# Two graph-attention layers on one core: the order of score and attention products in a step, some moved work in the opening, and the banks of the last row

## The chip, the cores and the metric

The kernel runs on one core of a Trainium2 chip. A core has five engines that run at the same time, each through its own queue in order: TensorE (PE in the profile; its weight loads are shown apart as PEld), VectorE (DVE), ScalarE (ACT), GpSimd (POOL) and SyncE (SP), which here issues the transfers between the chip's memory (DRAM) and the on-chip buffer. Matrix products land in PSUM, a small memory of eight banks for accumulation; everything else lives in the on-chip buffer of 128 partitions. The metric is the device time of the kernel in microseconds (us). A shorter time is better.

## The reference, cut to what matters

The input is x, 128 graphs of 128 nodes with 512 features each, and adj, a 128 by 128 mask for each graph. Two layers follow one another. Each is masked attention over the nodes, a residual addition and a layer normalisation:

```
x = layernorm(x + attention_0(x, adj))   # 4 heads of 64, no norm before, mask = adj
x = layernorm(x + attention_1(x, adj))   # 8 heads of 64, layernorm with gamma and beta before, mask = adj or self
attention: q, k, v = x W;  s = q k^T / 8;  s = where(mask, s, -big);  p = softmax(s);  out = (p v) Wo + bias
```

Everything is float32.

## The kernel before, in words

**Tiling.** Two graphs make a group, so there are 64 groups (NG). One group's 256 rows go through layer 0 and some steps later through layer 1. All products with weight matrices use a seven-product scheme for two-by-two blocks (Strassen's): seven half-size products, numbered 1 to 7, in place of eight, paid for with sums and differences of blocks. `sums` (L312) and `out_sums` make those of the rows on GpSimd (line 324), `weight_sums` (L202, `combine` at L211, line 214) those of the weights, once. A product accumulates into one of three PSUM banks, called a, c and f after the table `INTO`, and products 1, 6, 7, 4 follow one another in bank a, 5 and 3 in bank f. Between two of them an engine reads the bank: a product that goes on in a bank must wait until the earlier value has been read.

**Steps.** The program is written out as one sequence, and each engine gets its instructions in that order; nothing reorders them. `opening` (L809) loads and transposes weights and takes groups 0 and 1 through the first stages. `step(s)` (L852) then runs for s = 2 to 63, and `closing_a`, two of `closing_b` and `last` finish the pipeline. A step works on several groups at once, which are at different stages: the layer 0 projections of group s (`product_0`, line 477), the scores of group s-1 in layer 0 (part 0) and of group s-4 in layer 1 (parts 1 and 2, one per graph), the attention products of group s-2 in layer 0 (part 0) and s-5 in layer 1 (parts 1 and 2), the layer 1 projections of group s-3 (`qk` and `v`, line 361), and the output projections of groups s-2 and s-5 (`out_product`, line 517). Parts 1 and 2 of the attention products therefore exist from step 5 on.

**Scores and attention products.** `scores` (L532) makes eight short products a part (16 records in the profile, two for each product): q of 64 features by k of 64 features, so that only 64 of the array's rows are used; even heads use the upper half, odd heads the lower. Part 0 is line 550; parts 1 and 2 are line 556. Parts 0 and 2 take two PSUM banks each from a pool of four (tag mm), part 1 takes the banks a0 and f0. `attend` (L656, products on line 679) multiplies the probabilities with v, again in eight products a part: here 128 rows are used but 64 columns. Part 0 goes to bank a, part 1 to bank f, part 2 to one of the pool. ScalarE copies the results out (lines 682 and 684). For the step the order of these products is:

```
made = scores(s, 0)
attend(s, 1)
made.update(scores(s, 1, 2))
...
attend(s, 0, 2)
```

`masked` (line 585, VectorE) writes the scores where the mask is set, `maxima` (line 591, VectorE) takes the row maxima, `exps` (line 600, ScalarE) the exponentials and their sums, `normalised` (lines 608 and 609, VectorE and GpSimd) divides, and `blocks` and `probs_arrive` turn the probabilities over through DRAM for the next step; `blocks_direct` (L642) does that on TensorE instead. `with_self` (L561, line 564) adds the diagonal to the mask for layer 1.

**What comes into the scores of layer 1.** Queries and keys of a group are written to DRAM and fetched back in another order by `kq_arrive` (L417) at the end of a step. `q_in_order` (L422, line 426) then has ScalarE copy the queries of both graphs into the tiles qo0 and qo1, and the next step's parts 1 and 2 of the scores read them.

**Residual rows.** `addend` (L694, line 701, GpSimd) adds a bias to the rows of a group, `out_product` adds the projections to them on VectorE (line 521), `stats` and `roots` make mean and scale (lines 712 to 735), and `flush` (L57) emits the normalisations that were queued (line 746, ScalarE).

**The end.** For the last group, `out_plain` (L760, line 769) makes each graph's output rows as two plain halves of 256 columns, both in one PSUM bank; `add_plain` (L772, lines 779 and 780) adds each half to the row and takes its statistics, `root_plain` and `norm_plain` (lines 784 to 793) finish and store the row.

Of the kernel before, what the change touches and what calls it, by code (L numbers as in the profile page):

```python
# [10 lines left out]
F32 = mybir.dt.float32  # L11
# [6 lines left out]
P = 128  # L18
# [9 lines left out]
def kernel(ctx: ExitStack, tc: tile.TileContext, x, adj, wq, wk, wv, wo, bo,  # L28
                            gamma, beta, w_qkv, w_out, b_out, out):
    nc = tc.nc  # L30
# [15 lines left out]
    ps_st = ctx.enter_context(tc.tile_pool(name="ps_st", bufs=1, space=PSUM))  # L46
# [97 lines left out]
    wo1 = const.tile([P, INNER[1] // P, E], F32, name="wo1")  # L144
# [167 lines left out]
    def sums(l, g):  # L312
        if not 0 <= g < NG:
            return
        xs = XS[l, g] = one.tile([P, 4, KH, N], F32, tag=f"xs{l}", name=f"xs{l}_{g}")
        halves_sums(xs, XT[l, g].rearrange("p (h c) (b n) -> p b h c n", h=2, b=2))
# [10 lines left out]
    XS, ACC, EV = {}, {}, {}  # L327
# [197 lines left out]
    SM, TOTAL, NMAX, PT, AT, SO = {}, {}, {}, {}, {}, {}  # L525
# [6 lines left out]
    def scores(s, *parts):  # L532

        made = {}
        for part in parts or PARTS:
            g = group_of(s, part)
            if g is None:
                continue
            if part == 1:
                ps = [ps_st.tile([P, 512], F32, tag=t, name=f"sc{part}_{g}_{t}") for t in ("a0", "f0")]  # L540
            else:
                ps = [mm_tile(f"sc{part}_{g}_{i}") for i in range(2)]
            ps = [x.rearrange("p (k n) -> p k n", n=N) for x in ps]
            if part == 0:
                for b in range(G):
                    for h in range(HEADS[0]):
                        r = slice((h % 2) * D, (h % 2 + 1) * D)
                        k_ = (qkv0[r, b, h // 2, 2].rearrange("p (a j) -> p a j", j=32) if g in PLAIN_0 else
                              RAW[0][r, :, 1, b * K0 + h // 2])
                        nc.tensor.matmul(ps[h % 2][:, b * K0 + h // 2, :].rearrange("p (a j) -> p a j", j=32),  # L550
                                         qkv0[r, b, h // 2, 1], k_, start=True, stop=True)
            else:
                b = part - 1
                for h in range(HEADS[1]):
                    r = slice((h % 2) * D, (h % 2 + 1) * D)
                    nc.tensor.matmul(ps[h % 2][:, h // 2, :].rearrange("p (a j) -> p a j", j=32),  # L556
                                     QO[g, b][r, h // 2], KQ[r, :, 0, b, h // 2], start=True, stop=True)
            made[part] = ps
        return made

    def with_self(g):  # L561

        if 0 <= g < NG:
            nc.vector.tensor_tensor(M[g], M[g], eye[:, None, :].to_broadcast([P, G, N]), op=ALU.max)
# [29 lines left out]
    def exps(s, part, *halves):  # L594
        if group_of(s, part) is None:
            return
        sm, nmax, total = SM[part], NMAX[part], TOTAL[part]
        for i in halves:
            for k in range(K1):
                nc.scalar.activation(sm[:, i, k, :], sm[:, i, k, :], AF.Exp, bias=nmax[:, i, k:k + 1],  # L600
                                     accum_out=total[:, i, k:k + 1])
# [158 lines left out]
    def out_plain(g, b, *steps):  # L760

        n = E // 2
        if 0 in steps:
            ACC["op", b] = ps_st.tile([P, 512], F32, tag=("a0", "f0")[b], name=f"op_{b}")
        acc = ACC["op", b]
        for i in steps:
            h = slice(i * n, (i + 1) * n)
            for c in range(K1):
                nc.tensor.matmul(acc[:, h], AT[1, g][:, b, c], wo1[:, c, h], start=i == 0 and c == 0,
                                 stop=c == K1 - 1, skip_group_check=True)  # L770

    def add_plain(g, b, i):  # L772

        n = E // 2
        h = slice(i * n, (i + 1) * n)
        row = R[g][:, b, h]
        if i == 0:
            ST[b] = two.tile([P, 2, nc.vector.BN_STATS_DIM], F32, tag="st_last", name=f"st_last{b}")
        nc.vector.tensor_add(row, ACC["op", b][:, h], row)
        nc.vector.bn_stats(ST[b][:, i], row)  # L780

    def root_plain(b):
# [26 lines left out]
    def opening():  # L809

        sums(0, 0)
        cleared(1, 0)

        for t in (1, 0, 2):
            if t == 0:
                for h in range(2):
                    nc.vector.tensor_scalar_mul(w0[:, :, 0, h, :], w0[:, :, 0, h, :], SCALE)
            product_0(0, 1, 2, ts=(t,))
            weight_sums_0(t)
        product_0(0, 5, 6, 3)  # L820
        prepare(2)
        load(2)
        product_0(0, 7)
        prepare(2)
        product_0(0, 4)
        transposed(1)
        load_quarters(2)
        sums(0, 1)

        made = scores(1)  # L830
        masked(made, 1, 0)
        maxima(1, 0)
        weight_sums_out(0)
        product_0(1, 1, 2)
        exps(1, 0, 0, 1)
        prepare(2)
        normalised(1, 0)
        product_0(1, 6, 5)
        prepare(2)
        addend(0, 0)  # L840
        product_0(1, 7)
        prepare(2)
        blocks_direct(1, 0)
        cleared(2, 0)
        weight_sums(w1qk, wsqk, 0)
        product_0(1, 3)
        prepare(2)
        product_0(1, 4)
        transposed(2)
        sums(0, 2)  # L850

    def step(s):  # L852

        made = scores(s, 0)
        attend(s, 1)
        made.update(scores(s, 1, 2))
        if s > 3:
            sums(0, s)
            arrive(s - 3)
        flush()  # L860
        load_ahead(s + 1)
        load_rows(s - 1)
        masked(made, s, 0, 1, 2)
        attend(s, 0, 2)
        maxima(s, *((0,) if s == 4 else (0, 1)))
        if s == 3:
            turn(s - 3)
            arrive(s - 3)
        out_sums(0, s - 2)
        if s == 3:  # L870
            sums(0, s)
            with_self(s - 3)
        exps(s, 0, 0)
        product_0(s, 1)
        exps(s, 0, 1)
        out_product(0, s - 2, 1, 2, *(() if s == 2 else (5,)))
        maxima(s, *((1, 2) if s == 4 else (2,)))
        product_0(s, 2)
        if s == 2:
            out_product(0, s - 2, 5, 6)  # L880
        normalised(s, 0)
        out_product(0, s - 2, *(() if s == 2 else (6,)), 3)
        exps(s, 1, 0)
        stats(0, s - 2, 0)
        product_0(s, 6)
        exps(s, 1, 1)
        out_product(0, s - 2, 7)
        (blocks_direct if s == 2 else blocks)(s, 0)
        product_0(s, 5)
        out_product(0, s - 2, 4)  # L890
        normalised(s, 1)
        finish(s - 3, 0)
        stats(0, s - 2, 1)
        exps(s, 2, 0)
        product_0(s, 7)
        finish(s - 3, 1)
        exps(s, 2, 1)
        if s > 2:
            probs_arrive(s, 0)
        blocks(s, 1)  # L900
        product_0(s, 3)
        if s == 3:
            weight_sums(w1qk, wsqk, 1)
        product_0(s, 4)
        transposed(s + 1)
        turn_qk0(s)
        if s in (2, 3):
            prepare(len(setup) - (s == 2))
        normalised(s, 2)
        qk(s - 3, 1)  # L910
        if s == 2:
            prepare(1)
        flush()
        if s > 2:
            probs_arrive(s, 1)
        qk(s - 3, 2)
        blocks(s, 2)
        arrive_qk0(s)
        qk(s - 3, 6)
        if s == 3:  # L920
            weight_sums(w1v, wsv, 0)
        if s == 4:
            weight_sums_out(1)
        qk(s - 3, 5)
        flush(latest)
        addend(1, s - 5)
        out_sums(1, s - 5)
        qk(s - 3, 7)
        if s == 3:
            weight_sums(w1v, wsv, 1)  # L930
        qk(s - 3, 3, 4)
        kq_arrive(s - 3)
        probs_arrive(s, 2)
        out_product(1, s - 5, 1, 2)
        v(s - 3, 1, 2)
        if s > 2:
            turn(s - 2)
        cleared(s + 1, 0, 1, 2)
        v(s - 3, 6)
        out_product(1, s - 5, 6, 5)  # L940
        v(s - 3, 5)
        out_product(1, s - 5, 7, 3, 4)
        q0_in_order(s)
        q_in_order(s - 3)
        addend(0, s - 1)
        v(s - 3, 7)
        stats(1, s - 5, 0)
        v(s - 3, 3)
        stats(1, s - 5, 1)
        v(s - 3, 4)  # L950
        if s > 2:
            with_self(s - 2)
        if s == NG - 1:
            arrive(s - 2)
            addend(1, s - 4)
# [162 lines left out]
    for s in range(2, NG):  # L1118
        step(s)
# [33 lines left out]
```

## Time and profile before

| | us |
|---|---|
| median of 3 runs | 2761.13 (2759.78 to 2761.82) |
| the profiled execution's own time | 2759.77 |
| its span, first to last instruction | 2758.0 |
| TensorE busy (PE) | 2743.3 |
| VectorE busy | 2033.5 |
| GpSimd busy | 1752.0 |
| ScalarE busy | 1506.1 |
| granted TensorE clock, share of full | 0.999 |

Times in the profile are counted from the first instruction. A row of the timeline gives start, duration, engine, line, operation, result and operands by the program's names, shapes (for a product: the size of the stationary operand, then the moving one) and how many records it joins; a bracket at its end says how long the engine had been idle before and what released it. Ends of matrix products are modelled by the profiler, so their starts are the better clock: the time of a stage below is the distance from its first start to the next stage's first start. The step s = 33, in the middle of the run, starts its scores at 1315.74 and the next step at 1358.23; periods of 42.49 and 42.35 us alternate from step 5 to step 62.

### The profile page before, as it was taken

Reading aid. Unit: us, or ns where it says so; the run is one execution under the profiler, and the core shown is the slowest. Engines: PE = TensorE matmul, PEld = TensorE weight load, DVE = VectorE, ACT = ScalarE, POOL = GpSimd, SP = SyncE. Lnnn points to the kernel's source line nnn. Section 1 sums busy time; section 2 is a strip of 40 time slices with the busy share of each in tenths; the row PEclk is TensorE's granted clock in tenths of the full one; section 3 lists DMA queues with packets and bytes.
Section 4 is the critical chain, followed back from the end, with each engine's and each line's share of the span. In section 5 each row is a group of like instructions: output and inputs, shape, how many; then the busy total and the mean of one; then the engine's idle time right before and its main releaser. Section 6 shows DMA issues by size and latency. Waiting matters only on the chain.

```text
span 2758.0 us, 49315 instructions
## 1 busy us (share of the span) xinstructions
PE 2743.3 (99%) x15811; PEld 2032.5 (74%) x15811; DVE 2033.5 (74%) x3671; ACT 1506.1 (55%) x4804; POOL 1752.0 (64%) x2311
## 2 busy tenths in 40 slices
PE   9999999999999999999999999999999999999998
PEld 8867767677776677776776767777767777677688
DVE  6777777777777777777777777777777777777765
ACT  3456465464564654645646546456465464564654
POOL 5565666666656666666566666665666666656664
PEclk9999999999999999999999999999999999999999
DMA  6567777777777777777777777777777777777652
GB/s 179 154 200 206 218 217 204 218 210 215 212 202 219 216 204 219 210 216 209 205 217 217 204 219 210 214 213 203 216 218 203 215 214 215 211 204 220 201 150 65
DMA packets 550290, 562.73 MB, mean 204 GB/s; under 512 B 55560, under 2 KB 468752, under 8 KB 550032
## 3 DMA queue, kind: packets, MB, share of 16 engines
q1 hardware_dynamic: 550032, 559.58, 71.5%
q8 instruction: 127, 2.08, 0.3%
q14 instruction: 131, 1.07, 0.1%
HBM read 300.95 MB, written 258.47 MB: 203 GB/s over the span
## 4 chain that ended last, share of the span: by engine, by line
PE 97%; DMA 1%; DVE 1%; issue 0%; SPq 0%; ACT 0%; POOL 0%; POOLq 0%; DVEq 0%; ACTq 0%
PE qka L361 16%; PE a L477 12%; PE oa L517 12%; PE va L361 8%; PE qkf L361 8%; PE av L679 7%; PE f L477 6%; PE of L517 6%; PE vf L361 4%; PE qkc L361 4%; PE oc L517 3%; PE c L477 3%; PE sc L550 2%; PE sc_a L556 2%; PE sc L556 2%; PE vc L361 2%
## 5 line engine op out<-in xcount | busy, mean ns | idle before, releaser
L600 ACT ACTIVATE sm<-sm,nmax 128x128 f32<-128x128 f32 x1536 | 594.8, 391 | 30.6 <-DVE nmax L591 27.9
L609 POOL TENSOR_TENSOR sm<-sm,rec 128x1024 f32<-128x1024 f32 x192 | 364.1, 1896 | 333.7 <-DVE rec L608 330.7
L701 POOL TENSOR_TENSOR r<-r,bias 128x1024 f32<-128x1024 f32 x128 | 301.5, 2356 | 130.9 <-ACT r L700 130.9
L521 DVE TENSOR_TENSOR r<-oa,r 128x256 f32<-128x256 f32 x508 | 211.1, 415 | 134.9 <-PE oa L517 129.4
L600 ACT ACTIVATION_READ_ACCUMULATOR sm<-sm,nmax 128x1 f32 x1536 | 291.4, 190 | 0.0
L371 ACT COPY ev<-va 128x256 f32<-128x256 f32 x128 | 47.6, 372 | 432.8 <-PE va L361 432.8
L627 DVE STREAM_TRANSPOSE turnedp<-sm 128x1024 f32<-128x1024 f32 x188 | 233.6, 1243 | 64.5 <-POOL sm L609 53.9
L720 POOL TENSOR_SCALAR ve<-mv 128x2 f32<-128x2 f32 x191 | 41.7, 218 | 371.4 <-DVE mv L713 360.9
L591 DVE TENSOR_REDUCE nmax<-sm 128x8 f32<-128x1024 f32 x192 | 226.6, 1206 | 0.3
L361 PE MATMUL qkf<-w,xs 128*128 128x512 f32 x472 | 221.8, 592 | 0.0
L361 PE MATMUL qka<-wsqk,xs 128*128 128x512 f32 x472 | 221.8, 592 | 0.0
L517 PE MATMUL of<-wo,so 128*128 128x256 f32 x760 | 205.9, 379 | 1.4 <-DVE r L521 1.0
L517 PE MATMUL oa<-wso,so 128*128 128x256 f32 x760 | 206.0, 380 | 0.4 <-DVE r L521 0.4
L324 POOL TENSOR_TENSOR xs<-xT 128x256 f32<-128x256 f32 x256 | 187.7, 733 | 22.4 <-DVE xT L118 18.6
L746 ACT ACTIVATE r<-r,shift,root 128x512 f32<-128x512 f32 x254 | 193.0, 809 | 2.5 <-POOL shift L735 2.5
L426 ACT ACTIVATE qo<-kq 128x512 f32<-128x512 f32 x118 | 67.9, 622 | 228.6 <-DMA kq<-scrkq 228.6
L324 POOL TENSOR_TENSOR so<-aT 128x256 f32<-128x256 f32 (+1 forms) x254 | 150.2, 591 | 52.1 <-ACT aT L682 44.6
L477 PE MATMUL f<-w,xs 128*128 128x128 f32 (+1 forms) x760 | 182.2, 376 | 0.2 <-DVE w L214 0.2
L477 PE MATMUL a<-ws,xs 128*128 128x128 f32 (+1 forms) x760 | 182.1, 375 | 0.0
L585 DVE COPY_PREDICATED sm<-m,sc 128x512 f32<-128x512 uint8 x256 | 172.4, 727 | 11.1 <-PE sc L550 2.2
L712 DVE BATCH_NORM_STATS2 st<-r 128x6 f32<-128x512 f32 x254 | 174.9, 689 | 2.3
L571 POOL MEMSET sm<- 128x1024 f32 x192 | 175.1, 952 | 1.4 <-DVE turnedp L627 1.4
(181 smaller groups left out, 6471.9 us busy)
## 6 DMA issues: line engine op xcount, KB each, us to landing
scrp<-turnedp SPq DMA_DIRECT2D x188, 512.0 KB, 3.6
pT<-scrp SPq DMA_DIRECT2D x752, 128.0 KB, 2.9
kq<-scrkq SPq DMA_DIRECT2D x236, 256.0 KB, 4.8
x<-in_x_dram SPq DMA_DIRECT2D x256, 128.0 KB, 4.0
r<-in_x_dram SPq DMA_DIRECT2D x64, 512.0 KB, 4.0
out_dram<-r SPq DMA_DIRECT2D x63, 512.0 KB, 3.6
scr<-turned SPq DMA_DIRECT2D x62, 512.0 KB, 6.7
kq<-scr SPq DMA_DIRECT2D x248, 128.0 KB, 2.8
```

The source lines that it names most:

```text
L324: nc.gpsimd.tensor_tensor(o, a0, a1, op=op)
L361: nc.tensor.matmul(o, lhsT, rhs, start=first and m == 0, stop=m == len(todo) - 1, skip_group_check=True)
L477: nc.tensor.matmul(o, lhsT, rhs, start=first and n == 0, stop=n == len(todo) - 1, skip_group_check=True)
L517: nc.tensor.matmul(acc, left[:, c], right[:, c], start=first and c == 0, stop=c == hk - 1, skip_group_check=True)
L521: nc.vector.tensor_add(part, acc, part)
L591: nc.vector.tensor_reduce(NMAX[part], SM[part], AX.X, ALU.max, negate=True)
L600: nc.scalar.activation(sm[:, i, k, :], sm[:, i, k, :], AF.Exp, bias=nmax[:, i, k:k + 1], accum_out=total[:, i, k:k + 1])
L609: nc.gpsimd.tensor_tensor(SM[part], SM[part], rec[:, :, :, None].to_broadcast([P, 2, K1, N]), op=ALU.mult)
L627: nc.vector.transpose(t.rearrange("p q (h r) -> p q h r", r=32), SM.pop(part).rearrange("p i k (q r) -> p q (i k) r", r=32))
L679: nc.tensor.matmul(pm[i * D:(i + 1) * D, at, :].rearrange("p (a r) -> p a r", r=32), v, pT[:, :, i * K1 + at, :], start=True, stop=True)
L701: nc.gpsimd.tensor_tensor(R[g], R[g], (bias0, bias1)[l][:, None, :].to_broadcast([P, G, E]), op=ALU.add)
L746: nc.scalar.activation(R[g][:, b], R[g][:, b], AF.Identity, bias=shift[:, b:b + 1], scale=root[:, b:b + 1])
```

## The change

In each step all score products of the three parts are now issued first, and all attention products of the three parts after them, in the place where parts 0 and 2 stood. In the queues of the other engines this moves the copy of part 1 (line 684) behind the normalisations that `flush` emits and behind part 0's copy.

In the first steps several pieces of work have other places: the sums of group 2's rows (from the end of `opening` into step 2, behind `out_sums`), the diagonal of group 0's mask (from the first half of step 3 to its end), the exponentials of part 0 (in steps 2 to 4 behind the first projection product with its copy), the maxima of part 2 in step 4, `blocks_direct` in step 2, and the bias addition of group 2 in step 3.

At the end, the two halves of each of the last rows go to two PSUM banks each, so that the four halves use a0, a, f0 and f.

```diff
     def out_plain(g, b, *steps):
         n = E // 2
-        if 0 in steps:
-            ACC["op", b] = ps_st.tile([P, 512], F32, tag=("a0", "f0")[b], name=f"op_{b}")
-        acc = ACC["op", b]
         for i in steps:
-            h = slice(i * n, (i + 1) * n)
+            acc = ACC["op", b, i] = ps_st.tile([P, 512], F32, tag=(("a0", "a"), ("f0", "f"))[b][i], name=f"op_{b}{i}")
             for c in range(K1):
-                nc.tensor.matmul(acc[:, h], AT[1, g][:, b, c], wo1[:, c, h], start=i == 0 and c == 0,
+                nc.tensor.matmul(acc[:, :n], AT[1, g][:, b, c], wo1[:, c, i * n:(i + 1) * n], start=c == 0,
                                  stop=c == K1 - 1, skip_group_check=True)
...
-        nc.vector.tensor_add(row, ACC["op", b][:, h], row)
+        nc.vector.tensor_add(row, ACC["op", b, i][:, :n], row)
...
         prepare(2)
         product_0(1, 4)
         transposed(2)
-        sums(0, 2)
 
     def step(s):
-        made = scores(s, 0)
-        attend(s, 1)
-        made.update(scores(s, 1, 2))
+        made = scores(s)
...
         masked(made, s, 0, 1, 2)
-        attend(s, 0, 2)
+        attend(s)
...
         out_sums(0, s - 2)
-        if s == 3:
+        if s in (2, 3):
             sums(0, s)
-            with_self(s - 3)
-        exps(s, 0, 0)
+        if s > 4:
+            exps(s, 0, 0)
         product_0(s, 1)
-        exps(s, 0, 1)
+        exps(s, 0, *((0, 1) if s < 5 else (1,)))
         out_product(0, s - 2, 1, 2, *(() if s == 2 else (5,)))
-        maxima(s, *((1, 2) if s == 4 else (2,)))
+        maxima(s, 1 if s == 4 else 2)
...
         exps(s, 1, 0)
+        if s == 4:
+            maxima(s, 2)
         stats(0, s - 2, 0)
         product_0(s, 6)
         exps(s, 1, 1)
         out_product(0, s - 2, 7)
-        (blocks_direct if s == 2 else blocks)(s, 0)
+        if s > 2:
+            blocks(s, 0)
         product_0(s, 5)
+        if s == 2:
+            blocks_direct(s, 0)
         out_product(0, s - 2, 4)
...
         product_0(s, 3)
         if s == 3:
+            addend(0, s - 1)
             weight_sums(w1qk, wsqk, 1)
...
-        addend(0, s - 1)
+        if s != 3:
+            addend(0, s - 1)
...
-        if s > 2:
-            with_self(s - 2)
+        for g in {2: (), 3: (0, 1)}.get(s, (s - 2,)):
+            with_self(g)
```

## The prediction

> **What bounds the kernel now.** I read the page's head first, then the chain that ended last, the timeline of TensorE in a middle step, the same in two places where the order differs, and what the waits show.
>
> ```profile
> span 2758.0 us, 49315 instructions
> PE 2743.3 (99%) x15811; PEld 2032.5 (74%) x15811; DVE 2033.5 (74%) x3671; ACT 1506.1 (55%) x4804; POOL 1752.0 (64%) x2311
> PE 97%; DMA 1%; DVE 1%; issue 0%; SPq 0%; ACT 0%; POOL 0%; POOLq 0%; DVEq 0%; ACTq 0%
> ```
>
> TensorE is the bound: 99% busy, 97% of the chain. Work on other engines counts only where TensorE waits for it. But a busy TensorE isn't a full one, so I looked at the spacing of starts in step 33.
>
> ```profile
> 1315.74 1.16 PE L550 MATMUL sc<-rawqk,qkv 64*128 64x128 f32 x16
> 1316.83 1.09 PE L679 MATMUL av<-pT,v 128*64 128x128 f32 x16
> 1317.86 0.37 PE L556 MATMUL sc_a<-kq,qo 64*128 64x128 f32 x1
> ...
> 1318.85 1.06 PE L556 MATMUL sc<-kq,qo 64*128 64x128 f32 x16
> 1319.84 1.09 PE L679 MATMUL av<-pT,qkv 128*64 128x128 f32 x16
> 1320.77 1.04 PE L679 MATMUL av<-pT,v 128*64 128x128 f32 x16
> 1321.74 1.57 PE L477 MATMUL a<-w,xT 128*128 128x256 f32 x8
> ```
>
> From the first score to the first projection: 1.09 + 1.03 + 0.99 + 0.99 + 0.93 + 0.97 = 6.00 us. The same part costs more beside a part of the other kind (1.09) than beside its own (0.93). Steps 5 to 63 all show 6.00 (one shows 6.03). Step 4 has no attention products of layer 1, so there the three score parts already stand together; the first closing stage has the three attention parts together:
>
> ```profile
> 92.35 1.16 PE L550 MATMUL sc<-rawqk,qkv 64*128 64x128 f32 x16
> ...
> 94.23 1.06 PE L556 MATMUL sc<-kq,qo 64*128 64x128 f32 x16
> 95.22 1.09 PE L679 MATMUL av<-pT,qkv 128*64 128x128 f32 x16
> ...
> 2633.89 1.09 PE L679 MATMUL av<-pT,qkv 128*64 128x128 f32 x16
> 2634.82 1.92 PE L679 MATMUL av<-pT,v 128*64 128x128 f32 x32
> 2636.66 1.16 PE L550 MATMUL sc<-rawqk,qkv 64*128 64x128 f32 x16
> ```
>
> Three score parts: 95.22 - 92.35 = 2.87 us. Three attention parts: 2636.66 - 2633.89 = 2.77 us.
>
> **What the Trainium skill says.** "TensorEngine Tiling (Array Packing)", Key Properties: changing the tiling mode, not just the tile, drains TensorE. The trace agrees: scores are 64 rows by 128 columns, attention products 128 by 64, projections 128 by 128, and a switch shows some 0.1 to 0.2 us. "PSUM — Partial Sum Buffer", Terms: two engines must not touch one bank in the same quadrant at once; the trace has VectorE waiting for both halves of the last row (below). "SBUF — State Buffer", SBUF: two separate sides: GpSimd and two-input VectorE operations share a port as an exclusive lock. The trace shows a VectorE sum of 256 columns (line 214) at 2.57 us beside GpSimd's addition of line 701 (2.52), against 0.42 for its neighbour.
>
> **The steps.** The change leaves three kinds of runs, projections, scores, attention, projections: three switches in place of five. New length 2.87 + 2.77 = 5.64, say 5.65 us: 0.35 saved in each of 59 steps (5 to 63), 20.6 us.
>
> What could wait instead? Scores of part 1 now start 0.99 us after the step's first score (step 4: 93.34 - 92.35), not 2.12. They need qo0, which ScalarE copies once the fetched keys and queries have landed:
>
> ```profile
> 299.00 1.15 ACT L426 ACTIVATE qo<-kq 128x512 f32<-128x512 f32 x2 [5.57 <-DMA kq<-scrkq]
> ```
>
> The first of these two copies takes 0.62. This is step 9 (first score 297.61), the latest: its end is at +2.02. TensorE follows such a copy by 0.06 to 0.10, so it must end by about +0.91. In the 58 steps that have it the mean end is +0.31, and nine are later, by 0.34, 1.11, 0.13, 0.01, 0.41, 0.10, 0.35, 0.12, 0.60: 3.2 us. Nothing on the way from the key products to these copies is shortened, so I keep 3.2; with all of them 0.5 later it would be 9.5. qo1 is needed 0.9 later and comes 0.52 later: no cost. No transfer is moved, and SP's queue keeps its order.
>
> The copy of part 1's attention result now stands on ScalarE behind two normalisations (1.52) that start when GpSimd's shift is ready (line 735, +2.56 in step 33), then part 0's copy to about +4.7, part 1's to +5.2, part 2's to +6.35, 0.7 after the projections start. Behind them stand the exponentials, which now begin 1.1 after the projections start: still on time. The first reader on TensorE, `out_product` 1 on part 0, starts 1.4 after the projections, at +7.05: 2.3 spare. VectorE gains: it now waits 0.77 less for part 1's scores (48.0 us in total in the waits), so maxima end 0.4 earlier against TensorE. Bank a0, which the first projection needs, is read by +3.3. Cover is left everywhere: nothing.
>
> **Opening.** TensorE's waits there bound the gain:
>
> ```profile
> 45.95 0.67 PE L517 MATMUL of<-wo,so 128*128 128x256 f32 x2 [0.81 <-DVE r L521]
> 84.32 2.05 PE L361 MATMUL qka<-xT,wsqk 128*128 128x128 f32 x16 [0.44 <-DVE qo L444]
> 102.93 0.67 PE L517 MATMUL oa<-wso,so 128*128 128x256 f32 x2 [0.38 <-DVE r L521]
> ```
>
> Step 2, by the spacing of starts, loses 0.53 (GpSimd makes group 2's sums, 4 x 0.73, ahead of `out_sums`), 0.98 (VectorE's add waits for the projection's copy, 0.46, behind four exponentials) and 0.47 (the transposes of `blocks_direct` wait for GpSimd). Each is moved out of the way; 0.2 remains: 1.75 saved. Step 3: the mask (0.86 on VectorE) stands ahead of the adds that free banks, 0.21 + 0.35 saved; at its new place at the end VectorE idles 1.25 before line 585. The bias addition moves ahead of GpSimd's clears (2.73) to where VectorE transposes, so the 2.57 falls to 0.42 and the wait at 84.32 (0.60) goes. Step 4: 0.55 goes, since one maxima (1.2) leaves VectorE's way, but it lands ahead of the add that `out_product` 4 waits for: that add would end at about 105.05 and TensorE, there by 104.27, waits 0.9. Net loss 0.4. Sum 1.75 + 0.56 + 0.60 - 0.4 = 2.5 us; bounds -1 (the maxima costs twice that, the bias addition hits other sums) and 3.7 (all waits gone). The later exponentials in steps 2 to 4 cost nothing: ScalarE waits for the maxima there anyway.
>
> **End.**
>
> ```profile
> 2743.90 7.17 PE L769 MATMUL op<-wo,aT 128*128 128x256 f32 x32
> 2747.73 0.42 DVE L779 TENSOR_TENSOR r<-op,r 128x256 f32<-128x256 f32 x1 [4.25 <-PE op L769]
> ```
>
> Four halves take 4 x 1.72. VectorE waits for two, then the last row's chain is add 0.46, statistics, normalisation of the first row, add, statistics, aggregate at 2753.27. With own banks the first half of a row is added while the second is made: after 2751.11 only one add and one statistic (0.90) stand ahead of the aggregate, at 2752.01. Saved 1.25 us.
>
> **Sum.** 20.6 - 3.2 + 2.5 + 1.25 = 21.2 us. The profiled execution took 2759.77 (span 2758.0 and 1.8 around it), 1.4 under the median; from the median 2761.13 this gives 2740.
>
> **Rivals.** (1) Late queries: the wait eats a good part of the gain. For: 228.6 us of ScalarE waits on that transfer and a scatter of 2.6 us; against: mean slack 0.6. With copies 0.5 later and the opening at zero, 2761.1 - 20.6 + 9.5 - 1.25 = 2749. (2) The drain isn't saved: part of a switch is a change of operands or of the weight load's overlap, and TensorE keeps 6.00. For: the ends are modelled; against: starts in step 4 and at 2633.89 show it. Then only opening and end: 2757. (3) Slower: the same copies come later still, because the shorter step crowds the transfers (the queue's packets fill 71.5% of 16 engines). The waits are then 26.6 us for a shift of 1.0, about the whole gain of 24.4: beyond that the kernel is slower. With 1.1 it is some 31, so 2768. Against: the load rises by only 0.8%, and a stalled TensorE gives the transfers time.
>
> **How the numbers follow.** Forecast case 0.73, its own range 2734 to 2746 (waits 0 to 8, opening -1 to 3.7); rival 1 0.13; rival 2 0.06; rival 3 0.05; other 0.03. Low 2733; high 2751 takes in rival 1, leaving out the rest. 0.2% is 5.5 us, about what a measurement tells from no change: faster 0.90 (forecast, rival 1 and a part of the others), same 0.05 (rival 2 mostly), slower 0.05.
>
> **What would show it.** Right: 5.65 from first score to first projection in nearly all steps, periods of about 42.0 and 42.15, waits of `sc_a` on line 426 in about nine steps, no `sc_f` wait on VectorE, the last aggregate 0.9 after the last wait on line 769. Wrong: stages of 6.00; `sc_a` waits in most steps; `oa` waiting for line 682; opening waits over 2 us.

## The result, and the profile after

The changed kernel takes 2739.53 us (median of 4, 2738.9 to 2741.32) against 2760.73 for the kernel before on the same chip: a ratio of 0.9924, 95% interval 0.9907 to 0.9941. The forecast was 2740, so 21 us less. The head of the page of the changed kernel, with the shares of the engines in the chain of work that ended last:

```profile
span 2739.5 us, 49376 instructions
PE 2726.7 (100%) x15811; PEld 2033.4 (74%) x15811; DVE 2029.2 (74%) x3671; ACT 1505.2 (55%) x4804; POOL 1750.5 (64%) x2311
PE 97%; DMA 2%; DVE 0%; ACT 0%; SPq 0%; issue 0%; POOL 0%; POOLq 0%; ACTq 0%; DVEq 0%
```

TensorE has the same 15811 products and is still the bound. Its busy time itself fell, by 16.6 us. The timeline of TensorE in step 33 says where (most rows of the single products of part 1 left out):

```profile
1308.11 1.16 PE L550 MATMUL sc<-rawqk,qkv 64*128 64x128 f32 x16
1309.10 0.27 PE L556 MATMUL sc_a<-kq,qo 64*128 64x128 f32 x1
...
1309.21 0.27 PE L556 MATMUL sc_a<-kq,qo 64*128 64x128 f32 x1
...
1309.88 0.27 PE L556 MATMUL sc_a<-kq,qo 64*128 64x128 f32 x1
...
1309.99 1.06 PE L556 MATMUL sc<-kq,qo 64*128 64x128 f32 x16
1310.98 1.09 PE L679 MATMUL av<-pT,qkv 128*64 128x128 f32 x16
1311.91 1.92 PE L679 MATMUL av<-pT,v 128*64 128x128 f32 x32
1313.75 1.46 PE L477 MATMUL a<-w,xT 128*128 128x256 f32 x7
```

From first score to first projection: 1313.75 - 1308.11 = 5.64 us, where it was 6.00. In 49 of the 59 steps (5 to 63) the stage is within 0.03 of 5.65, and the step's period is 42.00 or 42.14 (0.02 to 0.05 more in three), where it was 42.35 or 42.49.

In the other ten steps the stage is longer. Over all 59 steps what lies above 5.649, the middle value, is 4.27 us; below this sum is called the excess. Here are ScalarE's copies of the queries in step 9 again, whose first score is at 296.45, and a row of the list of waits (total, times, longest). That list has only longer pauses, and TensorE's weight loads have a row of their own (3.1 us in 6 pauses):

```profile
297.68 1.15 ACT L426 ACTIVATE qo<-kq 128x512 f32<-128x512 f32 x2 [5.41 <-DMA kq<-scrkq]
PE sc_a L556 <- ACT qo L426: 1.6, 3, 0.7
```

The first of the two copies ends at +1.86 (counted from the step's first score), and part 1's scores start at +1.91 in place of +1.00: 1.08 lost in this step.

The opening in the timelines of TensorE (two rows) and VectorE (one):

```profile
47.29 0.67 PE L517 MATMUL of<-wo,so 128*128 128x256 f32 x2 [0.28 <-DVE r L521]
104.52 0.70 PE L517 MATMUL oa<-wso,aT 128*128 128x256 f32 x2 [0.73 <-DVE r L521]
82.31 0.69 DVE L444 SCALAR_TENSOR_TENSOR qo<-qka,eqk 128x512 f32<-128x512 f32 x1 [1.20 <-PE qka L361]
```

Of the waits in steps 2 and 3 one is left, 0.44 by the spacing of starts. At the queries' write (line 444) VectorE now waits for TensorE; before, TensorE waited for it. Step 4 has a new wait of 0.89. The last rows:

```profile
2726.67 7.17 PE L766 MATMUL op<-wo,aT 128*128 128x256 f32 x32
2728.77 0.42 DVE L776 TENSOR_TENSOR r<-op,r 128x256 f32<-128x256 f32 x1 [2.52 <-PE op L766]
2734.80 0.21 DVE L781 BATCH_NORM_AGGREGATE mv_last<-st_last 128x2 f32<-128x12 f32 x1
```

VectorE starts 2.1 us after the products' start, not 3.83, and the last aggregate comes 8.13 after it, not 9.37.

The two profiled executions differ by only 18.5 us of span (2758.0 and 2739.5), since the changed one lost 2.68 us ahead of its first score (24.81 against 22.13), where nothing was changed. The windows of both show why; the first row is that of before, the second of after, and the number behind the engines' busy times is the granted clock of TensorE:

```profile
11.00:18.00 7.00, 6.61 (x56) 6.42 (x57) 4.36 (x12) 1.43 (x3) 0.00 (x0) 1.00 1.11 289
```

```profile
11.00:18.00 7.00, 6.54 (x32) 6.54 (x33) 4.42 (x11) 0.71 (x2) 0.13 (x1) 0.53 1.11 296
```

After a pause near 9 us, in which TensorE waits for VectorE's work on the first weights, the clock was 0.53 for these 7 us in this execution. It is not the change's doing: the code up to the first score is the same in all kernels here but the one with idle products, and in the executions profiled below the clock was 1.00 or 0.76 in this stretch and the first score came between 22.0 and 24.2.

### The profile page after: what moved, and what is told of

The parts are those of the page before. It is cut to its first block, busy times and chain, and to the rows that moved or that the text cites. A ratio compares the mean times of both kernels' runs of the same rounds, so it can differ in the third digit from the quotient of the medians.

```text
span 2739.5 us, 49376 instructions
## 1 busy us (share of the span) xinstructions
PE 2726.7 (100%) x15811; PEld 2033.4 (74%) x15811; DVE 2029.2 (74%) x3671; ACT 1505.2 (55%) x4804; POOL 1750.5 (64%) x2311
## 4 chain that ended last, share of the span: by engine, by line
PE 97%; DMA 2%; DVE 0%; ACT 0%; SPq 0%; issue 0%; POOL 0%; POOLq 0%; ACTq 0%; DVEq 0%
PE qka L361 16%; PE a L477 13%; PE oa L517 11%; PE qkf L361 8%; PE va L361 8%; PE av L679 6%; PE f L477 6%; PE of L517 6%; PE qkc L361 4%; PE vf L361 4%; PE c L477 3%; PE oc L517 3%; PE sc L550 2%; PE sc L556 2%; PE vc L361 2%; PE sc_a L556 2%
## 5 line engine op out<-in xcount | busy, mean ns | idle before, releaser
L361 PEld LDWEIGHTS qkf<-w,xs 128*128 128x128 f32 x472 | 89.7, 190 | 112.9 <-issue 112.9
```

The costliest lines, as they stand in the source:

```text
L361: nc.tensor.matmul(o, lhsT, rhs, start=first and m == 0, stop=m == len(todo) - 1, skip_group_check=True)
```

## The experiments

The reasons to be told apart: (A) TensorE pays for every change of array shape, that is of the rows and columns that a product uses, and the step now has three (projections, scores, attention products, projections) in place of five; (B) the moved work of the opening and the new banks at the end bring the gain; (C) part 1's scores come earlier, which helps VectorE. Times are medians; the kernel before stood at 2761.2 to 2761.3 beside each group.

**The order of a step alone**, on the kernel before:

```diff
-        made = scores(s, 0)
-        attend(s, 1)
-        made.update(scores(s, 1, 2))
+        made = scores(s)
...
-        attend(s, 0, 2)
+        attend(s)
```

> The kernel before with the new order of a step alone (all scores, then all attention products); the opening and the last row stay as they were. If TensorE pays for each change of array shape (theory A), the stage from first score to first projection is 5.65 us in place of 6.00, 20.6 us in 59 steps, less some 4 us of waits for late queries: about 2744 against 2760.7. If the gain came from the moved work of the opening and the banks at the end (theory B), this kernel stays at about 2757 to 2761.

2743.64 us, ratio 0.9934 (0.9922 to 0.9947). The stage is 5.65 in most steps and its excess 6.05. Theory B falls for the bulk of the gain.

**The moved work and the new banks alone**: the changed kernel with the order of a step undone.

> The changed kernel with the old order of a step; the moved work of the opening and the new banks at the end stay. Theory A: the opening gives 3.0 and the end 1.25 us, so about 2756.5, and the stage is 6.00 again. Theory B: about 2740.

2757.8 us, ratio 0.9987 (0.998 to 0.9993), stages of 6.00; the 3.4 us are less than the 4.25 expected. The two parts gain 17.6 and 3.4 us, together 21.0; the whole change, 21.2. They add up.

**Five changes of shape, but early scores**, on the changed kernel:

```diff
-        made = scores(s)
+        made = scores(s, 0, 1)
+        attend(s, 1)
+        made.update(scores(s, 2))
...
-        attend(s)
+        attend(s, 0, 2)
```

> The changed kernel with the order scores 0 and 1, attention 1, scores 2, attention 0 and 2: as many changes of shape as before (five), but part 1's scores as early as in the changed kernel. Theory A: the stage is 6.00 plus the waits for late queries, about 3 to 4 us in all, so 2760. If it is the early scores of part 1 that help, by way of VectorE (theory C), the gain stays: about 2740.

2763.49 us, ratio 1.0008 (0.9999 to 1.0016): the gain is gone, and the kernel is no faster than before although it keeps the moved work. The stage is 6.00 in most steps and its excess (above 6.00) 5.24 us. So earlier scores alone (theory C) bring no gain, only the late queries. This was 3.5 us more than expected, some 2 of them for these waits, which I had put at 3 to 4.

**Four changes of shape**, on the changed kernel:

```diff
-        made = scores(s)
+        attend(s, 1)
+        made = scores(s)
...
-        attend(s)
+        attend(s, 0, 2)
```

> The changed kernel with attention 1 ahead of all scores, attention 0 and 2 behind them: four changes of shape, and the scores of part 1 start about 2 us after the step's start, as before. Theory A: half of the gain, a stage of about 5.83, and no waits for queries: about 2746 to 2747. Theory C: no gain in the steps, about 2756.

2749.12 us, ratio 0.9954 (0.994 to 0.9967). The stage is 5.80 with no excess worth naming (0.16 us), so the waits for queries go, as expected. The time is 2 to 3 us over the expectation: in nearly every step the weight loads of these attention products now wait 0.4 us or less for the read that frees bank f (line 386), 23.1 us of idle time in the list of waits. By the spacing of starts it costs only some 0.05 us a step: behind its stage a step lasts 36.41 or 36.55 us here, 36.35 or 36.49 in the changed kernel.

**Seven changes of shape**, with the same products: part 1's attention products cut into heads 0 to 3 and 4 to 7, one copy after both.

```diff
-        made = scores(s)
+        made = scores(s, 0)
+        attend(s, 1, heads=0)
+        made.update(scores(s, 1))
+        attend(s, 1, heads=1)
+        made.update(scores(s, 2))
...
-        attend(s)
+        attend(s, 0, 2)
```

> The changed kernel with part 1's attention products cut into two halves of four heads: scores 0, first half, scores 1, second half, scores 2, attention 0 and 2: seven changes of shape in place of three, the same products. Theory A (a price for each change of shape, some 0.17 us): the stage is about 6.35, 0.7 above the changed kernel, 41 us in 59 steps less the waits for late queries that go away: 2776 to 2781. If the number of changes doesn't matter, only where part 1's scores stand: about 2756.

2778.89 us, ratio 1.0062 (1.0045 to 1.0079). The timeline of a middle step on TensorE (in this kernel the attention products are on line 685; some rows of part 1's scores left out):

```profile
1324.40 1.16 PE L550 MATMUL sc<-rawqk,qkv 64*128 64x128 f32 x16
1325.50 0.66 PE L685 MATMUL av<-pT,v 128*64 128x128 f32 x8
1326.08 0.37 PE L556 MATMUL sc_a<-kq,qo 64*128 64x128 f32 x1
...
1326.30 0.27 PE L556 MATMUL sc_a<-kq,qo 64*128 64x128 f32 x1
...
1327.18 0.66 PE L685 MATMUL av<-pT,v 128*64 128x128 f32 x8
1327.76 1.16 PE L556 MATMUL sc<-kq,qo 64*128 64x128 f32 x16
1328.86 1.09 PE L685 MATMUL av<-pT,qkv 128*64 128x128 f32 x16
1329.78 1.04 PE L685 MATMUL av<-pT,v 128*64 128x128 f32 x16
1330.75 0.48 PE L477 MATMUL a<-w,xT 128*128 128x256 f32 x1
```

The stage is 1330.75 - 1324.40 = 6.35, and between the parts nothing is waited for. With the others the series is: three changes 5.65, four 5.80, five 6.00 (in two different orders), seven 6.35. That is 0.175 us a change over the whole of it, and it is what the kernel gained.

The starts also tell a change of shape from a change of operands and banks. Score products start in pairs. In the changed kernel (the timeline of its step 33 above) part 1 follows part 0, which has the same shape but other operands and banks: its pairs start 0.11 us apart from the first on (1309.10, 1309.21), and the step to part 2 takes the same 0.11 (1309.88, 1309.99). Here the same part 1 follows attention products, and its second pair starts 0.22 after the first (1326.08, 1326.30). What the array does in the added time no view shows.

**The bias addition back at its old place**, on the changed kernel:

```diff
         if s == 3:
-            addend(0, s - 1)
             weight_sums(w1qk, wsqk, 1)
...
-        if s != 3:
-            addend(0, s - 1)
+        addend(0, s - 1)
```

> The changed kernel with the bias addition of group 2 at its old place in step 3. If GpSimd's addition and VectorE's sums exclude each other, the last sum of the first block of line 214 takes about 2.5 us again (0.42 in the changed kernel) and TensorE waits some 0.5 us for the queries' write of line 444: 0.5 us longer, which only the trace can show.

2739.65 us in one execution, and neither the long sum nor the wait came back: step 3 lasts 33.05, as in the changed kernel (33.05). The expectation missed. GpSimd's addition starts at 79.94 here, and VectorE is through with that block of sums at 79.77.

**The mask back at its old place, then both.** The first has the new place of the addition, the second its old one:

```diff
         if s in (2, 3):
             sums(0, s)
+        if s == 3:
+            with_self(0)
...
-        for g in {2: (), 3: (0, 1)}.get(s, (s - 2,)):
+        for g in {2: ()}.get(s, (s - 2,)):
             with_self(g)
```

> The changed kernel with the diagonal of group 0's mask at its old place in step 3. The waits there for the adds that free banks come back, 0.35 to 0.56 us, and VectorE is 0.9 us later at the weight sums. With the bias addition at its new place the wait for the queries' write near 83 us stays away. Step 3 is 0.4 to 0.6 us longer than 33.05.

> The same, with the bias addition of group 2 at its old place too. If it was the earlier VectorE, and not the moved addition, that took the wait for the queries' write away, the wait of 0.6 us and a sum of 2.5 us come back only here: step 3 is about 1.0 to 1.4 us longer than 33.05, near the 34.47 of the kernel before.

2742.06 and 2741.68 us in one execution each. Step 3 lasts 33.76 with the mask back (0.71 more, expected 0.4 to 0.6; the two waits for the banks are there again, 0.21 and 0.43 by the spacing of starts) and 34.47 with both (1.42 more, just above the 1.0 to 1.4 expected, and the very length of before). The first of these executions also lost 1.4 us in step 2, which its edit does not touch, so the two totals say little. With both edits, VectorE and TensorE:

```profile
80.79 2.58 DVE L214 TENSOR_TENSOR wsv<-w,wsv 128x256 f32<-128x256 f32 x1
84.03 2.05 PE L361 MATMUL qka<-xT,wsqk 128*128 128x128 f32 x16 [0.44 <-DVE qo L444]
```

So either edit alone takes the wait at the queries' write away: the mask, because VectorE is ahead of GpSimd's addition; the addition, because it falls on VectorE's transposes. That the two exclude each other was right; that the addition's move was needed in this change was not.

The move even costs something. In the profiles of all ten kernels with the addition at its new place, what follows the stage in step 7 is 0.34 to 0.35 us longer than in the other odd steps; in the four with it at the old place (the kernel before, the one with the order alone, and the two here) it isn't. VectorE's read of bank a near the end of that step, first in the changed kernel, then in the one with only the addition moved back:

```profile
252.91 0.42 DVE L386 TENSOR_TENSOR v<-va,ev 128x256 f32<-128x256 f32 x1 [0.86 <-PE va L361]
251.23 0.42 DVE L386 TENSOR_TENSOR v<-va,ev 128x256 f32<-128x256 f32 x1 [0.51 <-PE va L361]
```

The read comes 1.49 us after its product's start in the first and 1.13 in the second, and TensorE waits for it. Why, the views don't show. With the mask moved, then, the addition's move saved nothing in step 3 and cost 0.35 us in step 7.

**The maxima of step 4 two places later**, on the changed kernel:

```diff
         exps(s, 1, 0)
-        if s == 4:
-            maxima(s, 2)
         stats(0, s - 2, 0)
         product_0(s, 6)
         exps(s, 1, 1)
         out_product(0, s - 2, 7)
+        if s == 4:
+            maxima(s, 2)
```

> The changed kernel with part 2's maxima of step 4 two places later, behind the add that the fourth output product waits for. The wait of 0.89 us near 104.5 goes, with nothing new in its place, since the exponentials that need these maxima come 3 us later: 0.9 us shorter in the trace. If the maxima's later end is what then counts, a wait for the transposes of part 2 shows up instead.

2740.54 us in one execution. The wait did not go; it moved, to where the last projection product of the step needs VectorE's read of bank a:

```profile
104.96 1.56 PE L477 MATMUL a<-ws,xT 128*128 128x384 f32 x4 [0.70 <-DVE qkv L493]
```

It is 0.87 by the spacing of starts, and step 4 lasts 35.80, as in the changed kernel (35.83). In that stretch VectorE's queue sets the pace: what is put ahead of one read delays the next.

**The query copies in halves**, on the changed kernel:

```diff
             for b in range(G):
-                nc.scalar.activation(q_tile(g, b).rearrange("p c (a j) -> p a c j", a=4), KQ[:, :, 1, b],
-                                     AF.Copy, scale=SCALE)
+                to = q_tile(g, b).rearrange("p c (a j) -> p a c j", a=4)
+                for c in (slice(0, K1 // 2), slice(K1 // 2, K1)):
+                    nc.scalar.activation(to[:, :, c], KQ[:, :, 1, b, c], AF.Copy, scale=SCALE)
```

> The changed kernel with each query copy of ScalarE (0.62 us) cut into two halves of two heads pairs, so that the first score products of part 1 need only the first half. They are then ready about 0.25 us earlier. If lateness of the queries is what is left of the stage's spread, the stages above 5.65 become fewer and their excess falls from 4.2 us in all to about 2: about 2 us shorter, 2737.5. If the excess comes from the transfers of keys themselves, nothing changes.

2738.31 us, ratio 0.9916 (0.9901 to 0.9931), which overlaps the changed kernel's interval. The excess of the stages is 3.29 us, not 2. Seven executions with whole copies and part 1's scores at that early place, in this order of a step, show 4.27, 4.37, 4.26, 5.80, 6.05, 4.97 and 4.32. So the halves probably help, by a microsecond or two (the kernel with three edits below, which has them too, shows 3.64), but the times can't tell it.

**Three edits together**: those halves, the maxima of step 4 at their place of before, and idle products in the opening's pause.

```diff
+                warm = mm_tile("warm")
+                for _ in range(10):
+                    nc.tensor.matmul(warm[:, :P], ident, ident, start=True, stop=True, skip_group_check=True)
```

> The changed kernel with three edits: each query copy in two halves, both late maxima of step 4 at the place they had before the change, and ten idle products in the opening's pause of TensorE near 9 us, whose result nobody reads. If the granted clock falls after that pause in some executions, it stays at full speed in all, and the first score of step 1 starts near 22 us in place of 22 to 24.8: up to 2.7 us, on average some 1.3. The maxima give 0.25 and the halves 1 us. Together about 2 to 3 us less than the changed kernel. If the clock's fall has another cause, only the last 1.2 us.

2740.32 us, ratio 0.9929 (0.9917 to 0.9942). The five executions took 2745.07, 2746.9, 2739.65, 2740.1 and 2740.32. The changed kernel on the same chip:

> The changed kernel itself once more, on the same chip as the kernel with three edits, to compare the two: 2739 to 2740.

2741.92 us, ratio 0.9925 (0.9911 to 0.9938), 2 us over the expectation and within the spread of the five (2737.76 to 2742.81). Three edits together are no better. The clock was 1.00 from 11 to 18 us in the profiled execution, but its first score came only at 23.1, where 22 was expected; this is one sample and shows no cause. That execution (the one of 2745.07) also shows what it lost in step 4, which lasted 40.79 in place of 35.83, on VectorE and TensorE:

```profile
116.53 2.84 DVE L214 TENSOR_TENSOR wso<-wso,wo 128x512 f32<-128x512 f32 x1
121.16 2.10 PE L361 MATMUL qka<-xT,wsqk 128*128 128x128 f32 x10 [3.55 <-DVE qo L445]
```

A sum that took 0.69 in the kernel before met GpSimd's bias addition (116.48 to 118.83) and took 2.84; VectorE had waited 2.69 for a transfer of turned probabilities ahead of it, and TensorE then waited for the queries' write. Some 3.2 us of the loss lie ahead of that product's start; the rest came behind it, at a granted clock of 0.66 from 121 to 126 us. Which of the three edits brought step 4 into that position, and whether the other long execution (2746.9) had the same, stays open. No version measured here is clearly faster than the changed kernel.

## Why the prediction was right

The steps of the sum against the two profiled executions (us saved; starts of the first score of each step mark the borders):

| | predicted | measured |
|---|---|---|
| steps 5 to 63, changes of shape, 59 x 0.35 | 20.6 | 20.64 |
| late queries in these steps | -3.2 | -4.27 |
| step 2 | 1.75 | 1.87 |
| step 3 | 1.16 | 1.42 |
| step 4 | -0.4 | -0.25 |
| end | 1.25 | 1.24 |
| ahead of step 1 (clock) | | -2.68 |
| all else | | 0.5 |
| sum | 21.2 | 18.5 |

**The changes of shape** carried the forecast, and both halves of the argument held: that the price hangs on the number of changes, and that the two places in the trace of before where parts of one kind stood together give it. One reading beside them was wrong, though the sum doesn't use it: 1.09 beside the other kind against 0.93 beside its own are a score part and an attention part, not the same part. Like with like, a score part takes 1.09 us between two changes, 0.99 with one and 0.89 with none (part 1 in the changed kernel, 1309.10 to 1309.99). The rule of the Trainium skill, "TensorEngine Tiling (Array Packing)", Key Properties, that a change of mode drains TensorE (empties it first), agrees with the series of four counts, which shows the price and not the drain itself; the page has no price. Rival 2 is out: 6.00 became 5.65, and other operands alone cost nothing.

**Late queries** were the right new wait at the right place, TensorE's part 1 behind line 426; its size was taken from one execution of before, and executions of the same order vary from 4.3 to 6.1. That is rival 1 in a small form. Its stronger form and rival 3 did not happen: over the same 58 steps the first copy ends at +0.28 us on average, where it was +0.31.

**The opening** came out near its sum, 3.04 against 2.5, but one step of it failed as a reason: "The bias addition moves ahead of GpSimd's clears (2.73) to where VectorE transposes, so the 2.57 falls to 0.42 and the wait at 84.32 (0.60) goes". The wait goes without that move, since the moved mask alone puts VectorE ahead. The new wait of step 4 was foreseen at 0.9 and is 0.89.

**The end** is the term with the best fit, 1.24, and rests on one reading: VectorE's first add used to start only when both halves were made, and now starts after one. The rule on banks that I cited ("PSUM — Partial Sum Buffer", Terms) was not tried.

**Not foreseen**: the clock's fall ahead of step 1, which varies between executions with the same code there, and most of the remaining 0.5: the first closing stage waited 0.91 us for its queries in the execution of before and not in that of after, and step 7 lost the 0.35 that comes with the bias addition's move. That the medians meet the forecast within 0.5 us is partly luck: single terms missed by up to 1.1 us, and the clock alone moves an execution by more than that.

## What to carry to other kernels

Where TensorE is the bound and never waits, look at the spacing of starts between runs of different array shape: the price of a change hides in the busy time, and sorting the same products by shape takes part of it out. Then ask which operand is needed earlier than before, and compare its ready times over all steps, not in one. An edit that looks needed may be covered by another in the same change, and may cost something steps later: undo each alone and both together, and compare all steps.

## What the runs showed of the hardware that was not expected

The granted clock of TensorE between 11 and 18 us, after a pause of 2 to 3 us, was 1.00, 0.76 or 0.53 with the same code up to the first score. The way from the end of the pause to the first score took 10.9 to 11.3 us in four executions at 1.00 (10.9 in that of before), 12.3 to 13.0 in eight at 0.76 (12.6 in the changed kernel's second profile) and 13.35 in one at 0.53 (its first). This is a spread of 2.5 us between executions, more than all edits to step 2 together were worth (1.87). What decides on the clock isn't shown.
